# A scan-and-attention kernel on one core: the last network in halves, a broadcast by a matmul, and moved weight scaling

## The chip, the cores and the metric

The kernel runs on one core of a Trainium2 chip. The metric is the device time of one execution in microseconds (us), as the median of several runs. Everything is float32, and a float32 matmul shows up in the trace as two passes, that is two MATMUL instructions.

## The reference

Two layers follow one another on 8 sequences (B = 8) of 512 steps with 256 features, each with a residual: x = x + norm(layer(norm(x))).

```
# layer 1: a selective scan over 512 channels with 16 states
xz = x @ in_proj_w.T;  xc = silu(conv(x_ssm) + conv_b)
dt_r, B, C = split(xc @ x_proj_w.T)                 # 1, 16 and 16 columns
dt = softplus(dt_r * dt_proj_w + dt_proj_b)
h_t = exp(dt * A) * h_{t-1} + dt * B * xc           # for each state and channel
y = (sum over states of h * C + xc * D) * silu(z) @ out_proj_w.T
# layer 2: attention with 16 heads, 8 experts each for values and outputs (top 2 chosen)
gv, go = gate(x, Wsel_v), gate(x, Wsel_o)           # sigmoid, masked to the 2 largest
v = einsum(x, gv, Wv);  att = softmax(rope(q) rope(k)^T / 8);  o = att @ v
src = norm(src + einsum(o, go, Wo)) * g1 + b1
out = norm(src + relu(src @ W1 + b1) @ W2 + b2) * g2 + b2'
```

## The kernel before, in words

Features or tokens lie on the 128 partitions, and most tiles are 128 x 2 x 512. For each sequence b there are five pieces of work. `front(b)` norms the input, projects it (`project`, weights `w_in` in a pool tag `w_m` of two buffers), convolves, and makes the row of step sizes and the 32 rows of B and C in `px`. These 33 rows are copied to `bcd`, written to device memory (`bc_d`, L433), and the step sizes' row is read back over all 128 partitions (`row`, L443). ScalarE then makes softplus from it: Abs and Exp into `u` (L457, L459), Ln into `ln` (L471), Relu into `dt` (L548). `mamba(b)` runs the scan in 32 steps of two states and 128 channels: ScalarE makes the decays `da` (L503), VectorE does the scan and multiplies by `ct`, and GpSimd issues two accumulating DMAs a step, which add the two states to `xc` (L566). For b = 0 TensorE makes the scan's inputs (`ps_u`, L541). `mamba(b)` ends with the output product `ps_out` (L676), two norms, the gates' scores and the choice of experts. `heads(b)` makes the output gate `go` and writes it to device memory (`go_d`).

`Pair` does attention for two heads: the projection `ps_qk` (L810, weights `wqk`), scores, softmax, transposes (`ps_pt`), values (`ps_v`), `attend` (`ps_o`, copied to `o`), then `weigh`: `o` times the gate rows `gb`, which a DMA spreads over the partitions, gives `og`. `add_output(k)` adds expert k to the running sum `ps_a` in PSUM (L983, weights `wo`). A sequence has eight pairs, and a pair's `add_output`s are run between the parts of the next pair (`ahead`). `feed_forward(b)` then adds the input to `ps_a` on VectorE (`acc`), transposes to tokens (`ps_acc`), norms, transposes back (`ps_tr_f`), does the two products (L1040, L1062), two more norms, and stores. For the last sequence nothing runs beside its last pair's `add_output`s and its `feed_forward`.

The weights of queries and keys are scaled once, at the start, by `later_constants`: for each of eight pairs a tile `wqk_s` is loaded, its query half is scaled on ScalarE (L289), and the tile is written to `wqk_d` (L290), from where the pairs load it (L806).

The order on TensorE, VectorE, ScalarE and GpSimd is written out when the kernel is built (`_Order`): a planner keeps a clock of TensorE and VectorE by fixed estimates and runs generators such as `front` and `mamba` between the pairs' parts; `yield t` says that a part's next piece is due t us later, and `Free` pieces cost VectorE nothing. Each engine runs its own list in that order and waits where a needed tile is not there. The DMA queue of SyncE (SP) is in order too: an issue that must wait for a buffer holds all issues behind it. Pools with `bufs` buffers give out tiles in rotation; `psum_a` has a single one.

Of the kernel before, what the change touches and what calls it, by code (L numbers as in the profile page):

```python
# [32 lines left out]
P = 128  # L33
# [182 lines left out]
def _layers(  # L216
# [4 lines left out]
    with ExitStack() as ctx:  # L221
# [44 lines left out]
        def later_constants():  # L266

            nc.sync.dma_start(out=w_sel, in_=wsel)
            nc.sync.dma_start(out=angle[:, :, 0, :], in_=rope)
            half_turn = half.tile([P, P], F32, tag="half", name="half_turn")  # L270
            nc.sync.dma_start(out=half_turn, in_=turn)
            nc.sync.dma_start(out=b1_t, in_=b1)
            nc.sync.dma_start(
                out=rows_t.rearrange("p r d -> p (r d)"),
                in_=rows[:, : 4 * D].to_broadcast([P, 4 * D]),
            )
            yield 8.0


            vector.tensor_reduce(sign, half_turn, AX.X, ALU.add)  # L280
            vector.tensor_scalar(angle[:, 1, 0, :], angle[:, 1, 0, :], sign, None, ALU.mult)

            for i in range(H // 2):
                w = wpool.tile([P, 2, ND, P], F32, tag="wqk", name=f"wqk_s_{i}")
                nc.sync.dma_start(out=w, in_=wqk[i])
                yield 6.0
                while i > 1 and 0 not in state:
                    yield Free(2.0)
                nc.scalar.mul(w[:, 0], w[:, 0], HP**-0.5)  # L289
                nc.sync.dma_start(out=wqk_d[i], in_=w)  # L290

# [23 lines left out]
        def front(b):  # L315
# [34 lines left out]
            def project(m, ps=None):  # L350

                w = wpool.tile([P, ND, 2 * P], F32, tag="w_m", name=f"w_in_{b}_{m}")
                nc.sync.dma_start(out=w, in_=m_in[:, :, m * P : (m + 2) * P])
                ps = banks(f"ps_in_{b}_{m}") if ps is None else ps
                for i in range(2):
                    for c in range(ND):
                        nc.tensor.matmul(
                            ps[:, i, :], lhsT=w[:, c, bass.ts(i, P)], rhs=xt[:, c, :],
                            start=(c == 0), stop=(c == ND - 1),
                        )  # L360
                pe(3.42)
                return ps
# [63 lines left out]
                states(px, range(NC))  # L426
                pe(3.42)
            if b == 0:
                ps = project(NC + 2)
            yield Free(0.05)  # L430
            bcd = half.tile([2 * NS + 1, S], F32, tag="half", name=f"bcd_{b}")
            nc.scalar.copy(bcd, px[: 2 * NS + 1, 0, :])
            nc.sync.dma_start(out=bc_d[b], in_=bcd)  # L433
            if b == 0:
                pb = banks("ps_b")
                for t in range(NT):
                    nc.tensor.transpose(
                        pb[:, 0, bass.ts(t, NS)], bcd[:NS, bass.ts(t, P)], ident[:NS, :NS]
                    )
                nc.scalar.copy(b_t.rearrange("p t n -> p (t n)"), pb[:, 0, : NT * NS])  # L440
                keep(2, ps)
            row = half.tile([P, S], F32, tag="half", name=f"row_{b}")
            nc.sync.dma_start(  # L443
                out=row, in_=bc_d[b][2 * NS : 2 * NS + 1, :].to_broadcast([P, S])
            )
            yield free(1.0)
            if b > 1:
                yield from gate()
            yield free(2.0)

            us, lns = [], []
            for m in range(0, NC, 2):
                u = tile_for(f"u_{b}_{m}", "og")
                for i in range(2):
                    nc.scalar.activation(u[:, i, :], row, AF.Abs, **step_size(m + i))  # L457
                yield free(1.4)
                nc.scalar.activation(u, u, AF.Exp, scale=-1.0)  # L459
                us.append(u)  # L460
                yield free(1.1)
            while b == 1 and at["step"] < steps - 1:
                yield Free(0.5)
            for u in us:
# [324 lines left out]
        class Pair:  # L789
# [3 lines left out]
            def __init__(self, b, pair):  # L793
                self.b, self.pair, self.id = b, pair, f"{b}_{pair}"
                self.xt = inputs_of[b]
                self.p, self.og = {}, {}

                self.done = set()

            def need(self, *what):  # L800
# [129 lines left out]
            def attend(self):  # L930


                self.need(*((of, t) for of in ("pt", "v") for t in range(NT)))
                po = banks(f"ps_o_{self.id}")
                for t in range(NT):
                    for j in range(2):
                        nc.tensor.matmul(  # L937
                            po[j * HP : j * HP + HP, 0, :], lhsT=self.v[:, j, t, :],
                            rhs=self.pt[:, j, t, :], start=(t == 0), stop=(t == NT - 1),
                        )  # L940
                pe(4.4)
                self.o = one.tile([P, 1, S], F32, tag="o", name=f"o_{self.id}")
                nc.scalar.copy(self.o, po[:, 0:1, :])  # L943
                for q in range(2):
                    after(0.8 + 0.1 * q, lambda q=q: self.weigh_soon(q))

            def weigh_soon(self, q):
# [5 lines left out]

            def weigh(self, q):

                gb = wpool.tile([P, 2, S], F32, tag="gb", name=f"gb_{self.id}_{q}")
                for j in range(2):
                    r = (2 * self.pair + j) * E + 2 * q
                    nc.sync.dma_start(
                        out=gb[j * HP : j * HP + HP].rearrange("p e s -> p (e s)"),  # L960
                        in_=go_d[self.b][r : r + 2, :].rearrange("e s -> (e s)")
                        .unsqueeze(0).to_broadcast([HP, 2 * S]),
                    )
                og = self.og[q] = work.tile([P, 2, S], F32, tag="og", name=f"og_{self.id}_{q}")
                vector.tensor_tensor(og, self.o.to_broadcast([P, 2, S]), gb, ALU.mult)

            def add_output(self, k):

                if self.pair == 0 and k == 0:
                    sums[self.b] = psum_a.tile([P, ND, S], F32, tag="sum", name=f"ps_a_{self.b}")  # L970
                pa, q, i = sums[self.b], k // 2, k % 2
                order_of.run(lambda: q in self.og)
                if i == 0:
                    w = self.wo = wpool.tile(
                        [P, 2, D], F32, tag="wo", name=f"wo_{self.id}_{q}"
                    )
                    for j in range(2):
                        nc.sync.dma_start(
                            out=w[j * HP : j * HP + HP],
                            in_=wo[2 * self.pair + j][:, q, :].rearrange("(i p) d -> p i d", i=2),  # L980
                        )
                for c in range(ND):
                    nc.tensor.matmul(  # L983
                        pa[:, c, :], lhsT=self.wo[:, i, bass.ts(c, P)], rhs=self.og[q][:, i, :],
                        start=(self.pair == 0 and k == 0),
                        stop=(self.pair == H // 2 - 1 and k == E - 1),
                    )
                pe(1.71)
                if i == 1 and q + 2 < E // 2:
                    after(0.05, lambda: self.weigh(q + 2))  # L990

        def feed_forward(b, pa):

# [90 lines left out]
            nc.sync.dma_start(out=out[b].rearrange("(t p) d -> p t d", p=P), in_=z)  # L1084
            finished.add(b)

# [24 lines left out]
                    part()  # L1114
                order_of.run()

        last = None
        with tc.manual_schedule(engines=MANUAL):
            first = front(0)
            order_of.start(first, 0, next(first))  # L1120
            order_of.start(mamba(0), 0)
            order_of.start(front(1), FIRST, 9.0)
            first_constants()
            order_of.run(lambda: 0 in scanning)
            order_of.start(later_constants(), NET)
            order_of.run(lambda: 0 in inputs_of)
            pairs = {}
            follow(-1, H // 2 - 1)
            for b in range(B):
                for pair in range(H // 2):  # L1130
                    now = pairs.pop((b, pair))
                    ahead(now, lambda: follow(b, pair))
                    if pair == 0 and b:
                        order_of.start(feed_forward(b - 1, sums[b - 1]), NET)
                    now.attend()
                    order_of.run()
                    last = now
            for k in range(E):
                last.add_output(k)
                order_of.run()  # L1140
            order_of.start(feed_forward(B - 1, sums[B - 1]), NET)
            order_of.run(lambda: not (order_of.queue or order_of.rest))


# [81 lines left out]
```

## Time and profile before

| | |
|---|---|
| three runs | 3694.61, 3695.3, 3702.96 us; median 3695.3 |
| the profiled execution | 3698.07 us, span in the profile 3696.3 us |
| TensorE busy | 3413.1 us (92%), mean granted clock 0.965 |
| VectorE busy | 3047.2 us (82%) |
| ScalarE, GpSimd busy | 1645.2 us, 1681.2 us (45% each) |
| DMA | 578.48 MB, 157 GB/s on average |

TensorE is the busiest engine, but it is not equally busy: in the first tenth of the span it has 50 to 80% of each slice, from there nearly all of it, and in the last 80 us it has gaps again. The stages are therefore read one by one: the start up to about 300 us, where VectorE's scan of sequence 0 and the DMA queues carry most; the middle, where TensorE and VectorE both are nearly full; and the end, where only sequence 7 is left.

### The profile page before, as it was taken

How to read it: one execution, taken by the hardware profiler on the slowest of the kernel's cores; microseconds unless marked ns; L12 is line 12 of the kernel's file. 1: busy time of each engine (PE TensorE's matmuls, PEld its weight loads, DVE VectorE, ACT ScalarE, POOL GpSimd, SP SyncE). 2: the span in 40 equal slices, each digit the busy share in tenths (PEclk: the TensorE clock that was granted, in tenths of full speed). 3: DMA queues.
4: the chain of work that ended last, by engine and by line, in shares of the span. 5: the costliest groups of instructions: out<-in, count | busy, mean ns of one | idle time of the engine just before them, and what ended most of it. 6: DMA issues, size and time to landing. Idle time of an engine off the chain costs nothing.

```text
span 3696.3 us, 34548 instructions
## 1 busy us (share of the span) xinstructions
PE 3413.1 (92%) x10956; PEld 1626.4 (44%) x10956; DVE 3047.2 (82%) x3190; ACT 1645.2 (45%) x2798; POOL 1681.2 (45%) x1593
## 2 busy tenths in 40 slices
PE   5768889999999999999999999999999999999996
PEld 3633334444344444444444544434444444445443
DVE  7878998799989898999989998899988998754443
ACT  5524443545543455344544446443653444332331
POOL 1415663354645545454454545355444556232230
PEclk7879999999999999999999999999999999999998
DMA  4937774576866768477755868568765777344431
GB/s 144 196 93 183 174 176 119 149 186 166 195 150 162 179 168 196 121 182 177 199 142 142 201 149 209 138 152 194 183 168 132 179 191 175 99 120 112 111 92 57
DMA packets 285604, 578.48 MB, mean 157 GB/s; under 512 B 37608, under 2 KB 124904, under 8 KB 285424
## 3 DMA queue, kind: packets, MB, share of 16 engines
q1 hardware_dynamic: 204656, 427.33, 40.0%
q0 software_dynamic: 80768, 148.95, 24.1%
q8 instruction: 89, 1.46, 0.2%
q14 instruction: 91, 0.75, 0.1%
HBM read 405.72 MB, written 21.51 MB: 116 GB/s over the span
## 4 chain that ended last, share of the span: by engine, by line
PE 47%; DVE 26%; issue 8%; DMA 7%; ACT 5%; POOL 5%; SPq 0%; DVEq 0%; POOLq 0%; ACTq 0%
PE ps_v L907 14%; PE ps_a L983 12%; DVE h L175 11%; PE ps_qk L810 5%; DMA xc<-h 5%; PE ps_s L848 4%; PE ps_o L937 3%; PE ps_pt L883 3%; DVE ve L175 2%; DVE og L175 2%; DVE low L175 2%; PE ps_f L1040 1%; DVE xs L175 1%; DVE hit L175 1%; POOL ve L923 1%
## 5 line engine op out<-in xcount | busy, mean ns | idle before, releaser
L983 PE MATMUL ps_a<-og,wo 128*128 128x512 f32 x2048 | 967.1, 605 | 32.8 <-DVE og L175 32.5
L907 PE MATMUL ps_v<-wv,xt 128*128 128x512 f32 x2048 | 946.8, 606 | 21.4 <-DVE y L175 13.2
L923 POOL TENSOR_TENSOR ve<-ve 128x512 f32<-128x512 f32 x256 | 425.3, 1661 | 1144.9 <-DVE ve L175 994.7
L863 ACT ACTIVATE p<-ps_s,low 128x512 f32<-128x512 f32 x512 | 347.3, 683 | 723.6 <-DVE low L175 723.1
L566 POOL DMA_DIRECT2D xc<-h x504 | 465.1, 1103 | 384.7 <-DMA xc<-h 174.6
L907 PEld LDWEIGHTS ps_v<-wv,xt 128*128 128x128 f32 x2048 | 385.6, 193 | 544.8 <-issue 484.2
L983 PEld LDWEIGHTS ps_a<-og,wo 128*128 128x128 f32 x2048 | 373.1, 192 | 506.4 <-issue 429.0
L175 DVE TENSOR_TENSOR_SCAN h<-da,h 128x1024 f32<-128x1024 f32 x228 | 541.0, 2373 | 10.2 <-ACT da L503 0.2
L872 ACT ACTIVATE p<-p,total 128x512 f32<-128x512 f32 x512 | 341.5, 714 | 260.8 <-DVE total L175 260.4
L175 DVE TENSOR_TENSOR og<-o,gb 128x1024 f32<-128x1024 f32 x256 | 319.7, 1269 | 130.3 <-ACT o L943 72.4
L175 DVE TENSOR_TENSOR ve<-ps_v,gv 128x1024 f32<-128x1024 f32 x256 | 311.4, 1216 | 126.5 <-PE ps_v L907 99.3
L889 ACT COPY pt<-ps_pt 128x1024 f32<-128x1024 f32 x256 | 256.9, 1005 | 356.5 <-PE ps_pt L883 355.2
L503 ACT ACTIVATE da<-dt,decay 128x511 f32<-128x511 f32 x512 | 339.7, 713 | 104.6 <-DVE h L175 101.8
L175 DVE TENSOR_TENSOR h<-bt,dtx 128x1024 f32<-128x1024 f32 x228 | 321.2, 1409 | 33.7 <-DMA xc<-h 28.6
L175 DVE TENSOR_TENSOR h<-h,ct 128x1024 f32<-128x1024 f32 x256 | 339.1, 1324 | 3.8
L175 DVE TENSOR_REDUCE low<-ps_s 128x2 f32<-128x1024 f32 x256 | 310.4, 1213 | 26.6 <-PE ps_s L848 25.6
L924 POOL TENSOR_TENSOR ve<-ve 128x256 f32<-128x256 f32 x256 | 319.2, 1247 | 20.1
L832 POOL DMA_DIRECT2D qk<-sin x256 | 204.7, 1212 | 264.5 <-DVE qk L175 127.2
L848 PE MATMUL ps_s<-qk 64*128 64x512 f32 x1024 | 294.2, 650 | 23.7 <-ACT p L863 12.8
L883 PEld LDWEIGHTS ps_pt<-ident,p 128*128 128x128 f32 x2048 | 239.5, 141 | 132.0 <-issue 94.8
L937 PE MATMUL ps_o<-pt,v 128*64 128x512 f32 x1024 | 248.3, 611 | 29.0 <-POOL v L925 16.4
L883 PE MATMUL ps_pt<-ident,p 128*128 128x128 f32 x2048 | 266.7, 273 | 7.6 <-ACT p L872 3.3
(134 smaller groups left out, 3340.3 us busy)
## 6 DMA issues: line engine op xcount, KB each, us to landing
gb<-go_d SPq DMA_DIRECT2D x512, 256.0 KB, 4.9
xc<-h POOLq DMA_DIRECT2D x504, 256.0 KB, 5.7
wv<-in_wv_dram SPq DMA_DIRECT2D x128, 512.0 KB, 5.7
wo<-in_wo_dram SPq DMA_DIRECT2D x512, 128.0 KB, 4.0
ct<-bc_d SPq DMA_DIRECT2D x64, 512.0 KB, 5.9
bt<-bc_d SPq DMA_DIRECT2D x57, 512.0 KB, 5.2
wqk<-wqk_d SPq DMA_DIRECT2D x64, 256.0 KB, 2.6
qk<-sin POOLq DMA_DIRECT2D x256, 64.0 KB, 4.7
```

What stands on the lines that cost most here:

```text
L175: return getattr(self.engine, name)(*args, **kw)
L503: nc.scalar.activation(das[k % 2][:, j, 1:S], dt[:, m, 1:S], AF.Exp, scale=decay[:, m, g + j : g + j + 1],)
L566: nc.gpsimd.dma_start(out=xc[:, k % NC, :], in_=hs[k][:, j, :], accum_op=ALU.add)
L848: nc.tensor.matmul(ps[:, j, :], lhsT=self.qk[feats, 0, bass.ts(t, P)], rhs=self.qk[feats, 1, :], start=True, stop=True,)
L863: nc.scalar.activation(p[:, j, :], ps[:, j, :], AF.Exp, bias=low[:, j : j + 1], accum_out=total[:, j : j + 1],)
L872: nc.scalar.mul(p[:, j, :], p[:, j, :], total[:, j : j + 1])
L883: nc.tensor.transpose(pp[:, j, bass.ts(i, P)], self.p[t][:, j, bass.ts(i, P)], ident)
L907: nc.tensor.matmul(ps[:, i, :], lhsT=self.xt[:, c, bass.ts(t + i, P)], rhs=self.wv[:, c, :], start=(c == 0), stop=(c == ND - 1),)
L923: nc.gpsimd.tensor_tensor(ve[:, :, 0:4], ve[:, :, 0:4], ve[:, :, 4:8], ALU.add)
L924: nc.gpsimd.tensor_tensor(ve[:, :, 0:2], ve[:, :, 0:2], ve[:, :, 2:4], ALU.add)
L937: nc.tensor.matmul(po[j * HP : j * HP + HP, 0, :], lhsT=self.v[:, j, t, :], rhs=self.pt[:, j, t, :], start=(t == 0), stop=(t == NT - 1),)
L983: nc.tensor.matmul(pa[:, c, :], lhsT=self.wo[:, i, bass.ts(c, P)], rhs=self.og[q][:, i, :], start=(self.pair == 0 and k == 0), stop=(self. ...
```

## The change

The diff has six parts.

1. In `front(0)` the step sizes' row is no longer read back from device memory. A tile of ones (one row) times the row of `bcd` on TensorE gives it over all partitions in PSUM (`ps_row`), and Abs and Relu read it there. All four Abs come first, then the Silu `keep(2, ps)`, then both Exp.
2. In `front(1)` the pieces that make Abs and Exp are due later and further apart.
3. `later_constants` takes its `wqk_s` tiles from the tag `w_m` instead of `wqk`, and for pairs 2 to 7 the wait stands before the load and is for the output gates of sequence 0 (`gated`) instead of its value gates (`state`).
4. For the last sequence `add_output` works in halves of 256 columns (`add_half`), and the residual input enters the sum as a product with the identity on TensorE.
5. The last pair weighs all four pairs of experts at once, two of them in tiles borrowed from the tags `ve` and `p`.
6. The last sequence's output products and network are written out by hand (`last_net`): its weights (`w_1`, `w_2`, `w_o`) and the residual `x1` are loaded ahead into tiles that the scan has left, the work goes by halves of 256 tokens, and the two halves alternate on the engines.

```diff
@@ later_constants
-                w = wpool.tile([P, 2, ND, P], F32, tag="wqk", name=f"wqk_s_{i}")
+                while i > 1 and 0 not in gated:
+                    yield Free(2.0)
+                w = wpool.tile([P, 2, ND, P], F32, tag="w_m", name=f"wqk_s_{i}")
                 nc.sync.dma_start(out=w, in_=wqk[i])
                 yield 6.0
-                while i > 1 and 0 not in state:
-                    yield Free(2.0)
@@ front
             if b == 0:
-                ps = project(NC + 2)
+                ones = half.tile([2 * NS + 1, P], F32, tag="half", name="ones")
+                nc.gpsimd.memset(ones, 1.0)
...
+                row = psum_a.tile([P, 2, S], F32, tag="sum", name="ps_row")[:, 0, :]
+                nc.tensor.matmul(
+                    row, lhsT=ones[2 * NS :], rhs=bcd[2 * NS :], start=True, stop=True
+                )
+                ps = project(NC + 2)
+                yield Free(0.05)
+                for m in range(0, NC, 2):
+                    us.append(tile_for(f"u_{b}_{m}", "og"))
+                    for i in range(2):
+                        nc.scalar.activation(us[-1][:, i, :], row, AF.Abs, **step_size(m + i))
+                keep(2, ps)
+                for u in us:
+                    nc.scalar.activation(u, u, AF.Exp, scale=-1.0)
...
+                yield free(12.0 if b == 1 else 1.0)
...
-                yield free(1.4)
+                yield free(3.5 if b == 1 else 1.4)
                 nc.scalar.activation(u, u, AF.Exp, scale=-1.0)
                 us.append(u)
-                yield free(1.1)
+                yield free(3.5 if b == 1 else 1.1)
@@ Pair.attend, weigh
-                for q in range(2):
+                for q in range(E // 2 if self.final else 2):
...
+                spare = self.final and q > 1
+                of, tag = (work, "ve") if spare else (wpool, "gb")
+                gb = of.tile([P, 2, S], F32, tag=tag, name=f"gb_{self.id}_{q}")
@@ Pair.add_output
+                if self.b == B - 1:
+                    for g in range(2):
+                        self.add_half(k, g, self.wo[:, i])
...
+            def add_half(self, k, g, w):
+                pa = sums[self.b].rearrange("p g (c s) -> p g c s", c=ND)[:, g]
+                if self.pair == 0 and k == 0:
+                    nc.tensor.matmul(
+                        pa, lhsT=ident, rhs=self.xt[:, :, bass.ts(g, S // 2)],
+                        start=True, stop=False,
+                    )
+                for c in range(ND):
+                    nc.tensor.matmul(
+                        pa[:, c, :], lhsT=w[:, bass.ts(c, P)],
+                        rhs=self.og[k // 2][:, k % 2, bass.ts(g, S // 2)],
+                        start=False, stop=(self.final and k == E - 1 and c == ND - 1),
+                    )
@@ last_net: the order that it writes out
+            first = ((rows_of(0), ALU.mult), (rows_of(1), ALU.add))
+            outputs(0, range(E))
+            outputs(1, range(2))
+            nc.scalar.copy(acc[0], pa[:, 0])
+            outputs(1, range(2, 4))
+            to_tokens(0)
+            outputs(1, range(4, E))
+            normed(0, *first)
+            nc.scalar.copy(acc[1], pa[:, 1])
+            features(0)
+            to_tokens(1)
+            hidden(0, 0)
+            normed(1, *first)
+            hidden(0, 4)
+            features(1)
+            for f in range(0, NF, 4):
+                hidden(1, f)
+            for g in range(2):
+                second(g)
```

In it `to_tokens` and `features` are four transposes each with a copy on ScalarE, `normed` is a norm with the given factors behind it, `hidden(g, f)` is 16 MATMULs of 256 columns (eight products in two passes) and four Relus, and is called twice per half, and `second(g)` is 32 MATMULs, the sum, two norms and the store of that half.

## The prediction

> **What bounds the kernel now.** I read the page first (busy slices and clock), then windows by stage, then the timeline of the first 300 us and of the last 85. TensorE's row in the slices is the bound: from slice 7 on it is full, at granted clock 0.9 or more, until the last slice; its first seven slices and the last have room.
>
> ```profile
> PE   5768889999999999999999999999999999999996
> PEclk7879999999999999999999999999999999999998
> DMA  4937774576866768477755868568765777344431
> ```
>
> So time can be won where TensorE or VectorE waits early (everything behind then moves up, since each engine's list is the same there) and in the tail, where nothing runs beside sequence 7. In between, an edit costs what it adds to TensorE. Three early waits lie where the change touches:
>
> ```profile
> 42.65 1.52 ACT L457 ACTIVATE u<-row,chan,w_dt 128x512 f32<-128x512 f32 x2 [0.95 <-ACT sz L374]
> 51.44 0.69 DVE L175 TENSOR_TENSOR u<-u,w 128x512 f32<-128x512 f32 x1 [4.44 <-ACT ln L471]
> ...
> 117.83 1.52 ACT L457 ACTIVATE u<-row,chan,w_dt 128x512 f32<-128x512 f32 x2 [3.88 <-DMA row<-bc_d]
> 123.10 2.29 DVE L175 TENSOR_TENSOR_SCAN h<-da,ps_u 128x1024 f32<-128x1024 f32 x1 [3.13 <-ACT da L503]
> ...
> 272.26 5.25 PE L810 MATMUL ps_qk<-xt,wqk 128*128 128x512 f32 x8 [5.51 <-DMA wqk<-wqk_d]
> 277.62 1.23 DVE L175 TENSOR_TENSOR sin<-ps_qk,angle 128x1024 f32<-128x1024 f32 x1 [6.74 <-PE ps_qk L810]
> ```
>
> Columns: start, busy us, engine, line, tiles, count, and in brackets the idle time before and its releaser. Each pair shows a late input and the VectorE wait behind it. The tail:
>
> ```profile
> 3624.61 0.67 PE L983 MATMUL ps_a<-og,wo 128*128 128x512 f32 x1 [0.25 <-DMA wo<-in_wo_dram]
> ...
> 3642.92 1.94 PE L300 MATMUL ps_tr_f<-ident,y 128*128 128x128 f32 x8 [8.71 <-DVE y L175]
> ...
> 3645.96 9.73 PE L1040 MATMUL ps_f<-yt,w 128*128 128x512 f32 x16 [1.10 <-ACT yt L1027]
> ...
> 3677.07 1.22 DVE L175 TENSOR_TENSOR y<-y,ps_f 128x1024 f32<-128x1024 f32 x1 [12.88 <-PE ps_f L1062]
> ...
> 3692.03 0.39 SPq L1084 DMA_DIRECT2D out_dram<-z  x1
> ```
>
> Products, then norms, then products, one waiting for the other. From the last `ps_o` (ends 3615.3) to the span's end are 81.0 us.
>
> **A, the row by TensorE (-2.5 us).** `bcd` is copied at 37.16. Before, write, read-back and a Silu put the first Abs at 42.65. Now: two passes at 0.43 and some 0.2 of handing over, 38.3; four Abs (1.52 per two, 3.0), 41.3; Silu 1.02, which waits for `ps_in`, pushed behind `ps_row` by 0.9 to 41.7, so 42.8; one table load 1.28 and two Exp at 1.06, 46.2; the copy of `b_t` 0.2; load 1.28 and first Ln 1.1, 48.9. VectorE's product comes at 48.95 in place of 51.44. `bt` was issued at 39.24 and lands 5.2 later, under this. Ends -1.5 to -3.
>
> **B, spacing in `front(1)` and moved loads (-0.6).** ScalarE's Abs sat 3.88 in its queue for the row, and `da` stood behind it; three scan steps later the row has landed: -3.1. Against it stand the transfers: between 80 and 190 us the DMA engines are nearly saturated.
>
> ```profile
> 90.00:100.00 10.00, 6.08 (x28) 5.17 (x29) 9.28 (x6) 5.66 (x11) 5.69 (x7) 0.83 1.07 222
> 180.00:190.00 10.00, 7.68 (x26) 4.38 (x27) 6.00 (x5) 5.95 (x7) 1.74 (x2) 0.83 0.98 266
> ```
>
> (Length, then busy time of PE, PEld, DVE, ACT, POOL, then clock, DMA share, GB/s.) The shared tag `w_m` puts two `w_in` loads, before issued at 33.15 and 43.42, behind the first `wqk_d` writes (79 and 87 us), and pair 1's `wqk` load comes early, too: with one `wqk_s` load moved away some 512 KB more in that stretch, at 200 GB/s 2.5 us, which VectorE pays where it waits for `xc` today (1.16, 2.71 and 3.93 us at 90.6, 175.3 and 189.7). Ends -3.1 (all hidden) to +4 (a late `w_in` for `ps_in` at 102 as well; it has about 2 us of slack). I take -3.1 + 2.5.
>
> **C, scaled weights (-6.7).** Pair 1's `wqk` load stood on SP behind `wqk_d` writes that waited for ScalarE; issued at 269.48, it held `ps_qk` 5.51 us, and then `ps_qk` ran 5.25 where 3.6 is usual, at half clock. In the new order the writes of pairs 2 to 7 wait for `gated`, behind that load. VectorE's 6.74 goes, and what follows (`go`, its write, `gb`, `og` at 298.99 after 7.99 idle) moves with it, as a chain. Ends -5.5 (the wait alone) to -7.1 (with a ScalarE scaling of 0.4 taken from `go`'s path).
>
> **D, the six writes moved (+0.5).** They come on SP at 305 to 346 ahead of `gb`, `wo`, `ct` and `wqk` issues, each after a scaling of 0.4 on ScalarE. Issues there run several us ahead of need; 0 to +2.
>
> **E, early loads (+3).** `w_1` and `w_2` (1 MB each) are issued at about 3113 and 3119, `w_o` (1 MB) at 3147, on queues that also carry the last scan's `xc`. `w_2` needs the tile of `dtx`, whose last reader starts at 3114.25 and takes 1.75; an issue of `w_2` that comes earlier holds SP, and behind it `gb` and `wv` issues, which land 4.9 and 5.7 us after issue and are due several us later; `w_o` needs `xc` free, behind `ps_out`.
>
> ```profile
> 3112.00:3118.00 6.00, 6.00 (x23) 2.87 (x22) 6.00 (x6) 3.34 (x7) 5.84 (x5) 1.00 1.03 261
> 3118.00:3126.00 8.00, 7.42 (x26) 3.50 (x25) 6.40 (x7) 5.46 (x12) 3.84 (x5) 1.00 0.66 143
> 3139.50 7.84 PE L676 MATMUL ps_out<-w_out,xc 128*128 128x256 f32 x28 [2.64 <-DVE xc L175]
> ```
>
> 2 MB at 250 GB/s is 8.4 us; up to 3140 there is idle share for about 3.5 of it; the rest delays `xc`, for which `ps_out` waits already. Taken in part, as `wv` and `wo` loads can give way: +3, ends 0 and +7. The page "DMA: Bandwidth & Descriptors" of the Trainium skill (Specifications) gives 358 GB/s as one core's share of device memory; by it 2 MB would take 5.9 us, by estimate, and E be nearer +2. The row's 261 GB/s at share 1.03 decides.
>
> **F, halves in sequence 7 (+2.4).** TensorE is 100% busy from 3200 to 3615. Two identity products in two passes add 2 x 0.86 = 1.72. Seven pairs' 224 MATMULs of 512 columns become 448 of 256. In full stretches 512 columns take 0.429; 256-column MATMULs with a weight load each (L1062 at 3332) came 32 in 6.91, 0.216. 448 x (0.2159 - 0.2144) = 0.7. Upper end 0.226 (the tail's L1062, 32 in 7.24): +5.2, with the identities +6.9.
>
> **G, the tail (-14.6).** Worked out from `ps_o`'s end: first product at 1.9 (as today); half 0 of eight experts 6.9, to 8.8; two and two experts of half 1, 12.3; transposes 12.9, copy 13.5; the rest of half 1 to 16.1. Half 0's norm and factors on VectorE and GpSimd (two stats 0.8, aggregates 0.4, GpSimd 1.03, scale 0.7, two factors 1.4, handing over) take 4.5, to 18.0; transposes and copy 19.3; `hidden(0)` 32 x 0.216 = 6.9, 26.2; features of half 1, the last four Relus 26.7 to 28.7; `hidden(1)` 35.7; `second(0)` 42.7; `second(1)` 49.7. VectorE then takes per half the sum 0.7, two norms, two factors and x1, 9.0 together: half 0 ends at 51.9, half 1 starts behind it, 60.9; the store 4.3 as today, 65.2. 81.0 - 65.2 = 15.8. The stalls on `wo` and `gb` (0.25 to 0.65 and 2.84 in the trace) go with the ahead-of-time loads: the `gb` of the last two pairs of experts are issued when GpSimd has read `ve` (3608.8) and the `p` tiles come free (near 3610), land near 3616, and are wanted at 3619.6; if they come later, today's 2.84 is back. Two gaps of about 2 us for TensorE are left (at 16 and 26.7). The rows: after 1.94 idle the clock stayed 1.00; after 2.64 `ps_out` took 7.84 for 28 (6.05 at full rate), +1.8; after 8.71 it was 0.50. I allow 1.2; ends 0 and 4, so -16 to -11.
>
> The skill's "TensorE: Matmul & The Clock Gate" (Part 1) has the clock fall only after an idle window of about 3.4 us; by it both gaps are free and the sum 1.2 lower. The 2.64 row speaks against it.
>
> **The sum.** -2.5 - 0.6 - 6.7 + 0.5 + 3 + 2.4 - 14.6 = -18.5. From the profiled execution (3698.07; span 3696.3) 3679.6; it stands 2.8 above the median of 3695.3, by which 3676.8. I say 3678. About 0.3% (11 us) is what a measurement of this kernel can tell from no change: faster is below 3684.2, slower above 3706.4.
>
> **Rivals.**
> - *The head gives nothing back to the end.* A, B and C are absorbed because the scan of sequence 0 is bound by transfers (share 0.98 at 180 to 190), or the `go` to `gb` chain starts late anyway: 9.8 less, 3688. For: `xc` waits of 3.93 at the end of scan 0. Against: C's wait lies behind that scan.
> - *The late loads hold TensorE* for 12 us, all of 2 and part of the third megabyte: E +12, 3687. For: share 1.03. Against: 0.63 to 0.86 behind it.
> - *Half-width MATMULs cost more than half* (slower). 448 in the busy stretch and 64 in the tail, 512 in all: with 0.28 each (`ps_out`'s row, 7.84 / 28) it is 512 x 0.064 = 33, the sum -18.5 + 33 = +14, 3709 by the median. It decides from 18.5 / 512 = 0.036 us more each, 0.25. Against: L1062 at 0.216 where TensorE is full.
> - *The change doesn't do what it says*: the new order may leave pair 1's load behind writes. The changed kernel's built order shows it ahead; 0.02, in the rest.
>
> **Numbers.** Forecast 0.64, head rival 0.14, load rival 0.12, half-width rival 0.06, rest 0.04. Terms' ends together reach from about -27 to +2; taking not all at once, the range is 3668 to 3692, which also holds the first two rivals. Faster: 0.61 of the forecast, 0.04 and 0.03 of the first two rivals: 0.68. Slower: 0.05 of the third, 0.03 of the rest: 0.08. Same: 0.24.
>
> **What would show it.** First Ln's product on VectorE near 49; no row wait near 118 and no `ps_qk` wait of 5 near 265; `xc` waits at the end of scan 0 not over 8 us in sum; `ps_out` of sequence 7 waiting under 6; L983 at 256 columns 0.214 to 0.218 from 3200 on; last `ps_o` to the end 65 to 67. Wrong: a tail over 70, half-width MATMULs over 0.23, or less than 6 us won by 300.

## The result and the profile after

| | before | after |
|---|---|---|
| first comparison, median | 3696.9 us (4 runs, 3694.6 to 3703.0) | 3676.5 us (4 runs, 3674.4 to 3677.7) |
| ratio | | 0.9944, 95% interval 0.9929 to 0.9958 |
| profiled execution's span | 3696.3 us | 3672.6 us |
| all runs of both kernels in this study | 42 runs, median 3695.2, 3686.2 to 3704.2 | 5 runs, median 3675.9, 3673.0 to 3677.7 |

The time fell by 20 us, and 3678 was forecast. The sum being right does not show that its terms are; most of what follows is about the terms, and about how much of a term one profile can show.

The page of the changed kernel, the rows that answer those shown of before:

```profile
PE   5768989989899999999999999999999999999997
PEclk8879999999999999999999999999999999999998
DMA  4928874577866767477865868568775778443440
```

They look nearly the same. The difference has to be read from the places where the change acts. The timeline of the start, in the same columns as before:

```profile
38.08 2.79 ACT L447 ACTIVATE u<-ps_row,chan,w_dt 128x512 f32<-128x512 f32 x4 [1.27 <-PE ps_row L439]
...
47.86 1.28 ACT L489 ACT_TABLE_LOAD   x1 [1.67 <-DMA sz_d<-sz]
...
50.24 0.69 DVE L175 TENSOR_TENSOR u<-u,w 128x512 f32<-128x512 f32 x1 [4.64 <-ACT ln L489]
```

Abs starts 4.6 us earlier than before (38.08 for 42.65), but VectorE's product only 1.2 (50.24 for 51.44): between them stands a wait that the forecast did not have. Further on, the scan of sequence 0 and pair 1's products:

```profile
98.45 2.29 DVE L175 TENSOR_TENSOR_SCAN h<-da,ps_u 128x1024 f32<-128x1024 f32 x1 [0.75 <-DMA xc<-h]
...
121.39 2.28 DVE L175 TENSOR_TENSOR_SCAN h<-da,ps_u 128x1024 f32<-128x1024 f32 x1
...
126.53 2.29 DVE L175 TENSOR_TENSOR_SCAN h<-da,ps_u 128x1024 f32<-128x1024 f32 x1 [1.60 <-DMA xc<-h]
...
267.20 3.70 PE L830 MATMUL ps_qk<-xt,wqk 128*128 128x512 f32 x8
...
271.64 1.20 DVE L175 TENSOR_TENSOR sin<-ps_qk,angle 128x1024 f32<-128x1024 f32 x1
```

The wait for `da` at 123 (3.13) is gone, and one for `xc` follows (1.60). Pair 1's `ps_qk` waits no more and runs at full clock, 3.70 for 5.25. The tail, on TensorE:

```profile
3606.15 10.59 PE L1031 MATMUL ps_a<-og,wo_last 128*128 128x256 f32 x40 [1.94 <-DVE og L175]
3617.41 1.99 PE L1031 MATMUL ps_a<-og,wo_last 128*128 128x256 f32 x8 [0.68 <-ACT acc_last L1226]
...
3626.33 8.86 PE L1197 MATMUL ps_f_last<-yt_last,w_last 128*128 128x256 f32 x32 [0.24 <-ACT yt_last L1190]
...
3637.33 7.17 PE L1197 MATMUL ps_f_last<-yt_last,w_last 128*128 128x256 f32 x32 [1.70 <-ACT yt_last L1190]
```

The two L1197 rows are the same 32 MATMULs for the two halves, 8.86 and 7.17 us. From the end of the last `ps_o` (3604.2) to the span's end are 68.4 us, against 81.0 before and 65.2 to 66.4 in the forecast.

Subtracting the two first profiles along the run gives a surprise. The changed kernel leads by 0.25 us at the end of scan 0, 6.0 at pair 1's `sin`, and 14.2 at 3060 us. Between 300 and 3060 the two run the same lists of instructions, and no term of the sum lies there: 8 us without a cause.

### The profile page after: what moved, and what is told of

The parts are those of the page before. It is cut to its first block, busy times and chain, and to the rows that moved or that the text cites. A ratio compares the mean times of both kernels' runs of the same rounds, so it can differ in the third digit from the quotient of the medians.

```text
span 3672.6 us, 35152 instructions
## 1 busy us (share of the span) xinstructions
PE 3405.9 (93%) x11250; PEld 1680.0 (46%) x11250; DVE 3046.2 (83%) x3198; ACT 1647.2 (45%) x2810; POOL 1677.8 (46%) x1597
## 4 chain that ended last, share of the span: by engine, by line
PE 47%; DVE 27%; issue 8%; DMA 7%; ACT 5%; POOL 5%; SPq 0%; DVEq 0%; POOLq 0%; ACTq 0%
PE ps_v L927 14%; DVE h L175 11%; PE ps_a L1011 9%; DMA xc<-h 5%; PE ps_qk L830 4%; PE ps_s L868 4%; PE ps_a L1031 3%; PE ps_o L957 3%; PE ps_pt L903 3%; DVE low L175 2%; DVE ve L175 2%; DVE og L175 2%; DVE xs L175 2%; DMA gb<-go_d 1%; PE ps_in L357 1%
## 5 line engine op out<-in xcount | busy, mean ns | idle before, releaser
L1011 PE MATMUL ps_a<-og,wo 128*128 128x512 f32 x1792 | 846.9, 606 | 28.4 <-DVE og L175 28.3
L1011 PEld LDWEIGHTS ps_a<-og,wo 128*128 128x128 f32 x1792 | 326.4, 192 | 442.2 <-issue 370.8
```

Source lines behind the costliest of these rows:

```text
L1011: nc.tensor.matmul(pa[:, c, :], lhsT=self.wo[:, i, bass.ts(c, P)], rhs=self.og[q][:, i, :], start=(self.pair == 0 and k == 0), stop=(self. ...
```

## Experiments

### Is the middle's 8 us the change's? (e1 to e4)

e1 and e2 are the two kernels as they are. e3 and e4 split the diff: e3 takes parts 1 to 3 of it (the functions `later_constants` and `front`), e4 parts 4 to 6 (`Pair` and `last_net`).

```diff
 e3: before.py + the hunks of later_constants and front
 e4: before.py + the hunks of attend, weigh, add_output, add_half, last_net and the main loop
```

e1: 

> The kernel before, unchanged, for a second profile. In the first pair of profiles the changed kernel leads by 6.0 us at 283 us and by 14.2 at 3060, though from 300 to 3060 both run the same lists of instructions; that is 8 us that no term of the forecast holds. Theory N (one execution's own scatter: TensorE's half-clock stretches, 60.4 us against 47.8 lost between 300 and 3100): this profile's time of half clock differs from 60.4 by several us, and its scans between 300 and 3060 lie some us off the first profile's, in steps of 0.8 and 1.7. Theory S (the change makes the middle shorter): this profile repeats the first within 1 us at every scan, half-clock loss 60 again.

e2: 

> The changed kernel, for a second profile. Theory N: the lead over the kernel before between 300 and 3060 us grows by another amount than 8, anything from 2 to 8. Theory S: by 8 again, half-clock loss 48 again. In both: 1.7 us before the first Ln while its tile's old content is being stored (DMA of sz_d), and the late w_in products at 103 us.

e3: 

> The kernel before with parts 1 to 3 of the change alone (row by TensorE, order of Abs and Exp, spacing in front(1), moved scalings). By the forecast A + B + C + D = -9.3: 3687.6. By the first profiles: the lead is 0.25 at the end of scan 0 and 6.0 at 283 us, so -6.3: 3690.6 under theory N. Theory S with the cause in the head: the lead grows by 8 more in the middle, -14: 3682.

e4: 

> The kernel before with parts 4 to 6 alone (halves, last pair's weighing, last network). By the forecast E + F + G = +3 + 2.4 - 14.6 = -9.2: 3687.7. By the first profiles: E about 0, F +3.0, G -12.6, so -9.6: 3687.3, with the middle as before (lead within 1 us of 0 at 3060 in the mean). If the middle's 8 us come from the tail's part (tags or loads), the lead is 8 already at 3060, and the time 3679.

Measured (e1 to e4 on one chip, e5 to e8 and e9 to e12 on two others, each group beside its own runs of the kernel before): e1 3691.7 and e2 3673.0 (one run each); e3 3685.8 (8 runs, ratio 0.9978, 0.9967 to 0.9989); e4 3682.7 (10 runs, ratio 0.9968, 0.9958 to 0.9977), against 3694.7 for the kernel before (17 runs). Marks that can be found in every profile, in us from the span's start (the ninth `low` is the softmax maximum that opens pair 2 of sequence 0; the 216th lies at the end of the middle):

| profile | scan 0 starts | 11th scan | 14th | 32nd | `sin` of pair 1 | first `og` | ninth `low` | from there to the 216th |
|---|---|---|---|---|---|---|---|---|
| before | 63.92 | 109.30 | 123.10 | 193.12 | 277.62 | 298.99 | 352.68 | 2770.28 |
| e1, before again | 64.14 | 109.63 | 124.62 | 194.99 | 281.30 | 303.13 | 356.48 | 2762.67 |
| e4, tail alone | 64.33 | 110.15 | 125.15 | 194.90 | 281.41 | 302.82 | 357.50 | 2764.72 |
| after | 62.74 | 110.80 | 121.39 | 192.87 | 271.64 | 293.04 | 346.35 | 2762.44 |
| e2, after again | 62.87 | 109.93 | 120.82 | 190.93 | 269.24 | 290.24 | 346.31 | 2764.91 |
| e3, head alone | 63.83 | 112.19 | 122.78 | 193.54 | 271.61 | 293.06 | 346.50 | 2765.09 |
| e9, as after up to the tail | 63.75 | 110.69 | 121.28 | 192.84 | 272.26 | 293.43 | 349.99 | 2765.02 |

The last column settles it. The kernel before took 2770.3 us for the middle in its first profile and 2762.7 in its second; the changed head gives 2762.4, 2764.9 and 2765.1. The 8 us were one execution's own: theory N holds, theory S fails. Summed over windows of 20 us, half-clock loss (time lost to a granted clock of 0.5) in that stretch was 57.4, 52.4 and 53.4 us for the old head and 45.6, 55.4 and 48.4 for the new, two ranges that overlap. Over all 14 profiles the two longest middles have the most of it (before, 57.4; e8, 60.2 in 2769.8 us) and the shortest the least (e7, 45.0 in 2759.8 us), so what scatters is at least in part TensorE's clock; what moves the clock there is not shown. From here on a term is the mean of three profiles against the mean of three, or of more. One mark alone can mislead: e9 differs from the changed kernel in the tail only, and its ninth `low` is at 349.99, so the changed head by itself gives 346.3 to 350.0 in four profiles (after, e2, e3, e9).

e3 and e4 add up: -8.9 and -11.9 make -20.8. Both ratios are clear of 1, so the head's gain and the tail's both reach the end. e4 lies 4.6 below its forecast of 3687.3, but that number stood on the 3696.9 of the first comparison; as a ratio the forecast was 0.9974 (9.6 less of 3696.9), inside e4's interval.

### The row by TensorE (e5, e11)

```diff
 e5
-row = psum_a.tile(...); nc.tensor.matmul(row, lhsT=ones[2 * NS :], rhs=bcd[2 * NS :], ...)
+row = half.tile([P, S], F32, tag="half", name="row_0")
+nc.sync.dma_start(out=row, in_=bc_d[0][2 * NS : 2 * NS + 1, :].to_broadcast([P, S]))
 e11
-spare = b == 0 and m
+spare = b == 0 and not m
```

e5: 

> The changed kernel, with the step sizes' row of sequence 0 read back from device memory again; the new order of Abs, Silu and Exp stays. The mark is the start of the first `low` of pair 0 of sequence 1 (346.3 to 346.5 us in three profiles with the new head, 352.7 to 357.5 in three without). Theory 1 (the forecast's A, whole): scan 0 starts 2.5 us later and keeps it, mark 348.9. Theory 2 (scan 0 is bound by transfers and gives it back): start 1.2 to 2.5 later, mark within 1 us of 346.4. Time within 3 us of 3676 either way.

e11: 

> The changed kernel with the two Ln tiles of sequence 0 exchanged: the first goes where nothing is stored from, the second into the tile whose store (sz_d) must land. Theory 1: the Ln's table load, which waited 1.67 us for that store, starts near 46.2; VectorE's first product of ln comes near 48.6 in place of 50.2, and scan 0 starts 1.0 to 1.6 us earlier (61.2 to 62 us). Theory 2 (another wait is as late): under 0.5 us earlier. No difference in the time that can be told, in both.

(The mark that the expectation of e5 calls the first `low` of pair 0 of sequence 1 is the ninth `low` of the table; it was misnamed.) The start of the span scatters by 1 us, so the time is counted from the copy of `bcd`:

| from the copy of `bcd`, us | Abs | VectorE's product | scan 0 |
|---|---|---|---|
| before, e1, e4 | +6.0 to 6.1 | +14.80 to 14.86 | +27.3 |
| after, e2, e3 | +1.85 | +13.70 to 14.29 | +26.2 to 26.8 |
| e5 | +5.98 | +15.97 | +28.5 |
| e11 | +1.85 | +12.36 | +24.9 |

e5: without the product of ones the start is 2.0 us later. Counted from the copy of `bcd`, scan 0's last step comes at +158.0 and `sin` at +237.2, later than in all four profiles of the changed head (+154.3 to 156.7 and +232.6 to 235.4). So far the 2 us are kept, as theory 1 has it; the mark itself, 349.2, lies inside those four's 346.3 to 350.0 and does not decide. The start is 1.1 later than in the kernel before, so the new order of Abs, Silu and Exp by itself costs time; only the row makes up for it. Time: 3672.2, 4 runs, ratio 0.9939 (0.9925 to 0.9954), not told apart from the changed kernel's.

e11: theory 1, scan 0 starts 1.6 us earlier. The timeline of its ScalarE:

```profile
42.94 1.02 ACT L374 ACTIVATE sz<-ps_in 128x1024 f32<-128x1024 f32 x1 [0.90 <-ACT u L447]
43.98 1.28 ACT L450 ACT_TABLE_LOAD   x1
45.27 2.00 ACT L450 ACTIVATE u<-u 128x1024 f32<-128x1024 f32 x2
47.18 0.19 ACT L456 COPY b_t<-ps_b 128x64 f32<-128x64 f32 x1
47.39 1.28 ACT L489 ACT_TABLE_LOAD   x1
```

The load follows the copy at once; the 1.67 are gone. The first Ln writes into the tile that `sz` was stored from. The change makes this Silu 1.1 us later (41.75 for 40.67), so its store (`sz_d`) lands later, and Ln waits for it. Time: 3675.0, no difference that can be told.

### Spacing in `front(1)` (e6)

```diff
-yield free(12.0 if b == 1 else 1.0)      -yield free(3.5 if b == 1 else 1.4)      -yield free(3.5 if b == 1 else 1.1)
+yield free(1.0)                          +yield free(1.4)                         +yield free(1.1)
```

e6: 

> The changed kernel with the old due times in front(1) (free 1.0, 1.4 and 1.1). Theory 1 (the row wait was worth its 3.1 us): ScalarE waits again for the row near 116, VectorE 3 us for `da`, and the mark is 349.5. Theory 2 (what the row wait no longer takes, the wait for xc takes): the VectorE waits at 120 to 130 change places and the mark moves by under 1 us.

```profile
121.22 1.52 ACT L475 ACTIVATE u<-row,chan,w_dt 128x512 f32<-128x512 f32 x2 [5.24 <-DMA row<-bc_d]
126.49 2.29 DVE L175 TENSOR_TENSOR_SCAN h<-da,ps_u 128x1024 f32<-128x1024 f32 x1 [4.48 <-ACT da L521]
```

The row wait is back, and longer (5.24; the row was issued at 117.17). From the 11th to the 14th scan are 15.2 us, as in e1 and e4 (15.0; 13.8 in before), against 10.6 to 10.9 in every profile with the spacing. Scan 0 ends at 195.35, 2.9 later than the mean of after, e2 and e3 (192.4), and the ninth `low` is at 352.5, later than in all four profiles of the changed head. Theory 1. Time: 3679.1, 4 runs, ratio 0.9953 (0.9934 to 0.9971), not told apart from the changed kernel's.

### The scaled weights (e7, e8, e10)

```diff
 e7: the lines of before (tag wqk; wait for `state`, behind the load)
 e8
-w = wpool.tile([P, 2, ND, P], F32, tag="w_m", name=f"wqk_s_{i}")
+w = wpool.tile([P, 2, ND, P], F32, tag="wqk", name=f"wqk_s_{i}")
 e10
+w = wpool.tile([P, 2, ND, P], F32, tag="wqk" if i < 2 else "w_m", name=f"wqk_s_{i}")
```

e7: 

> The changed kernel with the scalings of the query weights where they were (tag wqk, wait for `state` behind the load). Theory 1 (the forecast: C = -6.7, paid with 2.5 us of transfers in scan 0): ps_qk of pair 1 waits 5 to 6 us again near 270, the two w_in loads are early again; the mark is 346.4 + 6.7 - 2.5 = 350.6. Theory 2 (C's gain comes with no price): 353. Theory 3 (the head's gain is scatter of the kernel before): 346 to 347. Time +4 to +7 over the changed kernel for 1 and 2.

e8: 

> The changed kernel with its scaled tiles taken from the tag wqk again, but with the new wait for `gated` ahead of the load. The w_in loads of front(1) go out early again (near 33 and 43 us), and pair 1's load of wqk stays ahead of the late writes. Theory 1 (the late w_in and the traffic behind 80 us cost scan 0 its 2.7 us): VectorE's scan at 110.8 us starts 2 to 3 us earlier, the mark is 343.7 to 345, the time 1 to 3 below the changed kernel. Theory 2 (scan 0's end is set by its own transfers): the scan at 110 starts earlier, but the scans at 190 and the mark do not move by over 1 us.

e10: 

> The changed kernel with only the first two scaled tiles in the tag wqk; tiles 2 to 7 stay in w_m. The w_in loads of front(1) go out near 33 and 43 us, and the late scaled tiles do not need a pair's buffer. Theory 1 (the late run's loss of 8 us between 291 and 354 us came from SP waiting for a buffer of the tag wqk): scan at 108.7 us as there, pair 1's product near 270, the mark (first `low` of sequence 0's ninth set, 346.4 before) at 344 to 346, time 0 to 3 below the changed kernel. Theory 2 (the loss came from the earlier loads themselves): the mark is at 350 or later again.

| | 11th scan, from scan 0's start | 32nd scan | `sin` of pair 1, from the 32nd scan | ninth `low` | median, runs |
|---|---|---|---|---|---|
| before, e1, e4 | 45.4 to 45.8 | 193.1 to 195.0 | 84.5 to 86.5 | 352.7 to 357.5 | |
| after, e2, e3, e9 | 46.9 to 48.4 | 190.9 to 193.5 | 78.1 to 79.4 | 346.3 to 350.0 | 3675.9, 5 (after, e2) |
| e7 | 46.2 | 191.5 | 84.5 | 352.0 | 3680.6, 5 |
| e8 | 45.5 | 191.9 | 78.2 | 353.9 | 3681.4, 6 |
| e10 | 46.0 | 189.7 | 78.3 | 343.7 | 3670.8, 4 |

The ratios to the kernel before, 0.9962 (0.9948 to 0.9976) for e7, 0.9966 (0.9955 to 0.9978) for e8 and 0.9936 (0.9912 to 0.9960) for e10, overlap with the changed kernel's 0.9944 (0.9929 to 0.9958), so the times alone settle none of the three; the marks carry the reading.

e7 brings pair 1's wait back:

```profile
270.63 5.34 PE L830 MATMUL ps_qk<-xt,wqk 128*128 128x512 f32 x8 [5.36 <-DMA wqk<-wqk_d]
```

and with it 5 to 6 us between scan 0's end and `sin`, and the first `og` at 297.3 (290.2 to 293.4 in those four). So theory 3 is out. The mark is at 352.0, between theories 1 (350.6) and 2 (353), and one profile does not choose between them.

In e7, e8 and e10 the two `w_in` loads are early, and the ten scans are some 1 to 3 us shorter: the price that the changed kernel pays for the tag `w_m`. e8 keeps this and pair 1's early load as well, and was expected to win. By the marks it lost, between the first `og` (291.3, as the changed kernel) and the ninth `low`:

```profile
323.75 6.53 PE L830 MATMUL ps_qk<-xt,wqk 128*128 128x512 f32 x8 [5.75 <-DMA wqk<-wqk_d]
```

This is pair 2, waiting for a load that was issued at 319.38. In the changed kernel it was issued at 304.92. In SP's list of the changed kernel it stands behind the write of scaled tile 2; in that of e8 it stands behind those of tiles 3 and 4 too, each of which waits for its scaling. In the tag `wqk` the scaled tiles and the pairs' own stand in one line, and a pair's load comes when its turn does. Scan 0 ends in e8 no earlier than in the changed kernel (191.9), so e8's own theory 1 holds for the first scans only. e10 leaves only the first two tiles there. Scan 0 then ends at 189.7 and the mark is at 343.7, earlier than in any of the four, and so it is in e12 (189.3 and 344.7): theory 1 of e10.

### TensorE's clock in the tail (e9)

The nine profiles with the new tail, unfilled (after, e2, e4 to e8, e10, e11), have the same three gaps, 1.94, 1.74 and 1.70 us, and three lengths: 65.0 (e4), 66.7 (e2, e5, e7, e10, e11) and 68.4 us (after, e6, e8). The lengths differ by 1.69 us each, and so do the products behind a gap: 8.9 or 10.59 for the first, 7.17 or 8.86 for the second. Windows of the changed kernel, columns as before:

```profile
3604.20:3606.10 1.90, 0.01 (x1) 0.00 (x0) 1.23 (x2) 0.59 (x1) 0.00 (x0) 1.00 0.00 0
3606.20:3609.60 3.40, 3.40 (x9) 2.71 (x10) 3.30 (x3) 0.00 (x0) 0.00 (x0) 0.53 0.00 0
3609.60:3616.00 6.40, 6.40 (x31) 5.62 (x30) 0.00 (x0) 0.00 (x0) 0.00 (x0) 0.98 0.00 0
```

The granted clock is still 1.00 in the gap, 0.53 for the 3.4 us behind it, then full. The old tail has the same 1.94 us gap, and there too it sometimes costs: the 16 products behind it take 7.13 us in before and e1, 8.83 in e3. e9 fills the gaps with products that nobody reads:

```diff
+def warm(n):
+    ps = banks("ps_warm_last")[:, 0, : S // 2]
+    for k in range(n):
+        nc.tensor.matmul(ps, lhsT=w_o[:, k, 0, :P], rhs=w_1[:, 0, : S // 2], start=True, stop=True)
...
+warm(4)
 outputs(0, range(E))
...
+warm(3)
 features(0)
...
 features(1)
+warm(3)
```

> The changed kernel with products that nobody reads in TensorE's three gaps of the last stage: four (8 MATMULs of 256 columns, 1.73 us) before the first output product, three (1.3 us) before the first features, three before hidden(1). Seven profiles of the new tail show each gap costing either 0 or 1.69 us of half clock: the first gap (1.94 idle) in six of seven, the second (1.74) in three of seven, the third (1.70) in none. Theory 1 (the idle gap lowers the clock): with the gaps filled the first output products take 8.9 and hidden(0) 7.17, and last ps_o to the end is 65.0, against 66.7 and 68.4; time 1.5 to 3 us lower. Theory 2 (the half clock comes from elsewhere, by time of day of the throttle): the 1.69 us steps come all the same, and the fillings delay the work behind them by 0 to 1 us.

```profile
3608.45 1.99 PE L1210 MATMUL ps_warm_last<-w_last,wo_last 128*128 128x256 f32 x8
3610.46 8.90 PE L1031 MATMUL ps_a<-og,wo_last 128*128 128x256 f32 x40
...
3625.76 1.46 PE L1210 MATMUL ps_warm_last<-w_last,wo_last 128*128 128x256 f32 x6
3627.66 0.63 PE L1187 MATMUL ps_tr_f_last<-ident,y_last 128*128 128x128 f32 x4 [0.44 <-DVE y_last L175]
...
3628.97 7.17 PE L1197 MATMUL ps_f_last<-yt_last,w_last 128*128 128x256 f32 x32 [0.24 <-ACT yt_last L1190]
```

The products take 8.90 and 7.17, and the tail is 65.1 us, in e12 too: what theory 1 says, to the number. Nothing behind the fillers is late. Two such profiles could be chance, since e4 had no loss without fillers; but in all 14 profiles the 468 to 471 us ahead of the last `ps_o`, where TensorE has no gap over 0.86 us, ran at a granted clock of 1.00 throughout. So the gaps as the cause are likely; why one of them costs in one execution and not in the next is not shown. Time: 3670.8, 4 runs, ratio 0.9935 (0.9917 to 0.9952), not told apart from the changed kernel's.

### All three together (e12)

The diffs of e9, e10 and e11 in one kernel.

> The filled gaps, the two tiles of their own tag and the exchanged Ln tiles together. If the three gains stand and add (-2.3, -2, -1.2): 3670.5 against 3676 for the changed kernel. If the head's two are absorbed by the scan's own transfers: 3673.5. If the late load of w_in was only moved to another place: 3676.

Measured 3669.6 (5 runs, 3666.8 to 3674.4), ratio to the kernel before 0.9931 (0.9915 to 0.9946). Scan 0 starts at 61.6, its 11th scan is at 106.7 (110.8 in the changed kernel), the ninth `low` at 344.7. e10 alone had that mark at 343.7, so the 1.7 us of e11 do not show there: scan 0 ends at 189.3 in e12 and at 189.7 in e10. The median is the lowest of all, and 6 us below the changed kernel's 3675.9. The two were not run side by side, and the intervals of their ratios to the kernel before (0.9931 and 0.9944) overlap, so a gain over the changed kernel is likely rather than settled.

## Why the prediction was right, term by term

| term | forecast | measured | from |
|---|---|---|---|
| A, row and order of Abs and Exp | -2.5 | -0.8 | `bcd` to VectorE's product, 14.83 to 14.00 |
| B, late loads in scan 0 | +2.5 | +2.3 | scan 0's start to the 11th scan, 45.6 to 47.8 |
| B, row wait | -3.1 | -3.9, of which 1.4 come back as a wait for `xc` | 11th to 14th scan, 14.6 to 10.7; the next, 3.46 to 4.86 |
| A and B at scan 0's end | -3.1 | -1.9 | 32nd scan, 194.3 to 192.4 |
| C, pair 1's load | -6.7 | -7.4 | 32nd scan to `sin`, 85.8 to 78.4 |
| D, writes moved | +0.5 | +0.4 (one profile scatters by 3) | first `og` to the ninth `low`, 53.9 to 54.3 |
| E, early loads | +3 | +0.1 | 216th `low` to `ps_out`'s end, 22.9 to 23.0 |
| F, halves | +2.4 | +3.2, of which 0.85 a wait | `ps_out`'s end to the last `ps_o`, 467.95 to 471.14 |
| G, tail | -14.6 | -12.6 (after), -14.2 (mean of nine) | last `ps_o` to the end, 81.0 to 68.4; 81.3 to 67.1 |

Each measured number is the mean of three profiles against three (before, e1, e4; after, e2, e3), where not said otherwise. For E the old tail's three (before, e1, e3) stand against nine new (after, e2, e4 to e9, e11); F is the same to 0.01 us in all three old and all eleven new profiles; G's means are of before, e1, e3 and of the nine unfilled tails.

From scan 0's end on the measured rows (A and B, C, D, E, F, G by its mean) make -19.8, for -18.5 forecast and -19.3 to -20.4 by the medians. Two terms failed, with opposite signs: A won 1.7 less than forecast and E cost 2.9 less. That these nearly cancel is luck; the mechanisms of B, C and G are not. **A** was mis-sized by a wait that its sum did not have. The instructions together came out as counted: e11, where the wait is gone, has the product 12.36 us behind the start of `bcd`'s copy, and the forecast's 48.95 - 36.58 is 12.37. The step that failed is "the copy of `b_t` 0.2; load 1.28 and first Ln 1.1": the list of ScalarE was followed, but not what Ln's tile held before. A Silu that is moved moves its store, and the store keeps a tile. **E** failed at "the rest delays `xc`". The loads came where forecast (3098.5 and 3104.4, 14.5 us ahead of the forecast's 3113 and 3119, as all there is some 14), but `xc` was no later:

```profile
3098.00:3104.00 6.00, 6.00 (x22) 2.87 (x22) 6.00 (x6) 3.52 (x7) 5.68 (x5) 1.00 1.02 279
3104.00:3112.00 8.00, 7.42 (x25) 3.44 (x25) 6.40 (x7) 5.29 (x12) 3.99 (x5) 1.00 1.03 278
3112.00:3118.00 6.00, 6.00 (x15) 2.61 (x14) 3.29 (x5) 1.33 (x2) 4.61 (x7) 1.00 1.07 296
...
3123.78 1.23 DVE L175 TENSOR_TENSOR xc<-xc,sz 128x1024 f32<-128x1024 f32 x1 [4.70 <-DMA xc<-h]
```

and in the kernel before:

```profile
3138.22 1.23 DVE L175 TENSOR_TENSOR xc<-xc,sz 128x1024 f32<-128x1024 f32 x1 [4.96 <-DMA xc<-h]
```

The engines carried 278 to 296 GB/s at share 1.02 to 1.07, where 261 at 1.03 had been taken for full, and VectorE's wait for `xc` is 4.70 us, where it was 4.96. The second of the windows above is the stretch that before was 3118 to 3126, with 143 GB/s at share 0.66: the loads went there and into the next. A share of 1 was read as "no room", but it went with 261, 278 and 296 GB/s; that the traffic's make-up decides the rate is likely, not shown. "DMA: Bandwidth & Descriptors" of the Trainium skill (Specifications) gives about 358 GB/s of device memory per core; the 296 of 3112 to 3118, all traffic counted, is under that and above the 261 that was preferred. What is left of the rival "late loads hold TensorE" is nothing: E is +0.1.

The clock in **G** was allowed 1.2 us for two gaps; three gaps cost 0, 1.69 or 3.38, 2.1 in the mean of nine. The allowance had the right kind of number from a single row (2.64 idle, 1.8 lost); the row that it set against it (1.94 idle, clock 1.00) was one execution's, and the same gap costs 1.7 in e3. The sign "65 to 67" held in six of the nine. "TensorE: Matmul & The Clock Gate" of the Trainium skill (Part 1) has the clock fall after an idle window of about 3.4 us, and rise after as much busy time. The second half agrees: 1.69 us lost are 3.4 us at half clock. The first does not: behind gaps of 1.94 and 1.74 us it fell in eight and three of nine profiles, behind 1.70 in none.

**F** is 0.8 more than forecast, and the trace has it as a wait. From start to start the four identity MATMULs take 1.8 us and the 448 halves 0.5 more than 224 of full width, 2.3 together for 2.4 forecast. The rest is in sequence 6's network, in all eleven profiles with the new tail and in none with the old:

```profile
3291.61 1.04 PE L300 MATMUL ps_tr_f<-ident,y 128*128 128x128 f32 x8
...
3295.43 3.70 PE L1085 MATMUL ps_f<-yt,w 128*128 128x512 f32 x8 [0.85 <-ACT yt L1072]
```

Before, the same product follows without a wait:

```profile
3309.70 1.04 PE L300 MATMUL ps_tr_f<-ident,y 128*128 128x128 f32 x8
...
3312.60 3.70 PE L1040 MATMUL ps_f<-yt,w 128*128 128x512 f32 x8
```

ScalarE's copy `yt` starts 2.8 us behind the start of those transposes (3294.39), where it was 1.1 (3310.77), because it stands behind a softmax scaling, which here waited 2.21 us for VectorE and before 0.23. The rival of half-width MATMULs at 0.28 us is out: it would have made F some 30 us.

The first rival, the head's gain given back, was right in its mechanism for A and B (the loads in scan 0 and the new `xc` wait take back 3.7 of the 4.7 gained there) and wrong for C: e7 without it has 5 to 6 us back at `sin` and still at the first `og`. That gain reaches the end too: the head alone (e3) is 8.9 below the kernel before, with an interval clear of 1.

## What to carry to other kernels

Follow a moved instruction to its store, and the store to the tile that someone takes next: a Silu that came 1.1 us later put 1.7 us ahead of an Ln that is two steps further on. A tag is a queue as well: by single profiles the same scaled tiles cost 2 to 3 us in one tag (they push the next input weights back), some 7 in another (a pair's load comes behind two more of them), and neither when split between the two. Before a difference of two profiles is explained, profile each kernel a second time: here 8 of 24 us between the first two were one execution's own.

## What was not expected of the hardware

A gap of 1.94 or 1.74 us on TensorE costs either nothing or 1.69 us, from one execution to the next, and the clock still reads 1.00 inside the gap; with eight or six MATMULs in it, into a bank that nobody reads, it cost nothing in both profiles that had them (e9, e12). And one program's executions differ by some 18 us in 3695 (42 runs of the kernel before, 3686.2 to 3704.2; nine on one chip span all of it), with single stretches of equal work that differ by up to 7.6.
